# Seeding two PSUM sums from ScalarE in the second layer of a sparse graph network

## The chip, the cores and the metric

The kernel runs on one core of one Trainium2 chip. Its time is the device time of one execution, in microseconds (us). The kernel before was run three times: 926.32, 928.87 and 934.2 us, so its median is 928.87 us. A separate execution was taken by the hardware profiler; it lasted 933.13 us, and its trace spans 931.1 us from the first instruction to the last. All durations below come from that one trace.

A core has five engines that run side by side and meet at semaphores: TensorE (PE, matrix products), VectorE (DVE), ScalarE (ACT), GpSimd (POOL, which here issues the indirect transfers) and SyncE (SP, which issues plain transfers). Each runs its own list of instructions strictly in order. TensorE writes only to PSUM[...].

## The reference

Two graph layers on 3327 nodes with 512 features, each followed by a residual sum and a layer norm. Only the second one concerns the change. Here `adj` is 0/1, with some eight neighbours in a row besides the node itself:

```
type_sum = adj @ x
attn_a = sigmoid(concat(type_sum, x) @ Wa.T + ba)        # one number for each node
attn_b = sigmoid(concat(type_sum, x) @ Wb.T + bb)        # one number for each node
h = x @ W_sa
attn = row-normalised exp(-leaky_relu(s_left + s_right)) on the neighbours
x_a = attn @ h
x_b = adj @ (x @ W_gcnb) + b_gcnb
x = layernorm(x + sigmoid(attn_a * x_a + attn_b * x_b))
```

The kernel uses that sums over neighbours and projections can change places. For each node it forms a weighted sum of its neighbours' rows of `x`, with the weights `attn_a * attn`, and a plain sum of the same rows, scaled by `attn_b`. It projects the first with `W_sa` and the second with `W_gcnb`, both into one PSUM sum, and adds `b_gcnb * attn_b`.

## The kernel before

The nodes are sorted by their number of neighbours and cut into 26 tiles of 128. `CAPS[j]` says how many neighbour rows tile j holds, from 4 to 14; two of the tiles (`T0`, of 14 rows each) hold more in a shared "stair" row. After a first part that reads the adjacency matrix and does the first layer, the second layer begins about 532 us into the span.

Neighbour rows come by indirect transfers, one for each of the 226 rows and one for each of the two stairs. POOL issues them (line 615) into a ring of 42 row buffers; `gather()` issues as far as buffers are free. The own row of a node, `row1(j)`, is in SBUF from the first layer.

The loop `for i in range(NT + 3)` (lines 1150 to 1199) is a software pipeline written out by hand: in turn i, tile j is at position i of the order, j1 at i + 1, jp at i - 1 and jpp at i - 2. The order in the code is the order on each engine. In one turn:

- **ACT** takes the own score of j1 (`own_score`, line 1021), scales the plain sum of jp out of PSUM into `sp` (line 1159), copies the two transposed operands of jp out of PSUM (`sT`, line 1130), applies tanh to `za` of jpp (line 1169), does exp and tanh on the small weights of j1 (lines 1039 and 1054), finishes rows after a norm in some turns (line 1184), and at the end starts the weighted sum of j1 with the own row times its weight (`scaled_first`, line 1081).
- **PE** transposes the weighted and the plain sum of jp (`turn`, line 1128), adds the single rows of j into the PSUM sum `acc` by products with the identity (`plain_sum`, line 1118), projects jp's first half into `po` (`project`, line 1137), adds the sums of two rows of j that DVE has made, and projects jp's second half.
- **DVE** adds each row of j times its weight into `sw` (line 1097) and sums four or five pairs of rows in place (line 1099). Then come bias times gate plus projection for jpp (line 1167), the weights of j1 (lines 1032 to 1062, the last being what `scaled_first` waits for), the residual sum of jpp (line 1194) and its statistics (line 692), and after every few tiles a short chain that makes the norm's scale (lines 701 to 708).

The lines that the change touches stand thus in the loop:

```
sp = zs[jp, "sp"] = m1.tile([P, F], F32, tag="sp", name=f"sp{jp}")
nc.scalar.activation(sp, plain[jp], AF.Copy, scale=gates[jp][:, 1:2])
turn(jp, 0)
turn(jp, 1)
...
nc.vector.scalar_tensor_tensor(za, bias_g, gates[jpp][:, 1:2], proj[jpp], ALU.mult, ALU.add)
nc.scalar.activation(za, za, AF.Tanh, scale=0.5)
```

Both `acc` and `po` have two PSUM buffers that take turns from tile to tile. A product of 128x128 by 128x512 in float32 stands in the trace as two instructions (two passes).

Of the kernel before, what the change touches and what calls it, by code (L numbers as in the profile page):

```python
# [8 lines left out]
F32 = mybir.dt.float32  # L9
AF = mybir.ActivationFunctionType  # L10
ALU = mybir.AluOpType
# [3 lines left out]
P = 128  # L15
# [63 lines left out]
def sparse_pass(  # L79
# [39 lines left out]
    nc = tc.nc  # L119
    N, F = out.shape  # L120
    NP = x.shape[0]
    H, FO = a_self.shape
    KT = F // P
# [35 lines left out]
    ident = const.tile([P, P], F32, name="ident")  # L159
    ones = const.tile([P, P], F32, name="ones")  # L160
    bias0 = const.tile([P, F], F32, name="bias0")
    bias_g = const.tile([P, F], F32, name="bias_g")
# [13 lines left out]
    def place(j):  # L176

        return (0, j) if j < NG[0] else (1, j - NG[0])
# [5 lines left out]
    def row1(j):  # L184
        g, i = place(j)
        return x1[g][:, i, :]
# [468 lines left out]
    def gather():  # L655

        while waiting and waiting[0][0] - freed[0] <= RING:
            indirect(*waiting.pop(0)[1:])

    def free(j):  # L660

        freed[0] = ends_at[j]
# [78 lines left out]
    ws, accs, ws2 = {}, {}, {}  # L741
# [41 lines left out]
    def attend(j, lean, between):  # L783


        w = ws[j]
        acc = accs[j] = ps.tile([P, F], F32, tag="acc", name=f"acc{j}", bufs=2)
        if not lean:
            nc.tensor.matmul(acc, ident, bias0, start=True, stop=False)
        for s0, n, buf, o in got[j]:  # L790
            for s in range(s0, s0 + n):
                gv = buf[:, o + s - s0, 0:F].rearrange("p (h o) -> p h o", h=H)
                if s % 3 == 2:
                    for h in range(H):
                        nc.scalar.activation(gv[:, h, :], gv[:, h, :], AF.Copy, scale=w[:, s, h : h + 1])  # L795
                else:
                    nc.vector.tensor_tensor(  # L797
                        gv, gv, w[:, s, :].rearrange("p (h o) -> p h o", o=1).to_broadcast([P, H, FO]), ALU.mult
                    )
                row = buf[:, o + s - s0, 0:F]  # L800
                if lean and s == 0:
                    nc.vector.tensor_add(row, row, bias0)  # L802
                nc.tensor.matmul(  # L803
                    acc, ident, row, start=(lean and s == 0), stop=(s == CAPS[j] and j not in T0)
                )
                if s == 2:
                    between()
        if j in T0:
            gv = stair[j][:, 0:F].rearrange("p (h o) -> p h o", h=H)
            nc.vector.tensor_tensor(  # L810
                gv, gv, ws2[j].rearrange("p (h o) -> p h o", o=1).to_broadcast([P, H, FO]), ALU.mult
            )
            nc.tensor.matmul(acc, to_node, stair[j][:, 0:F], start=False, stop=True)
# [37 lines left out]
            rows_ready.append(j)  # L851

    rows_ready = []

    def put_rows():
        for j in rows_ready:
            scatter("table1", table1[:, :], own(j), row1(j), N - 1)
        rows_ready.clear()
# [3 lines left out]
    def open_pools():  # L862
        nonlocal gp, m0, ps, ring
        psf.release()
        pj.release()
        gp = ctx.enter_context(tc.tile_pool(name="gp", bufs=1))
        m0 = tc.alloc_tile_pool(name="m0", bufs=2, side="left")
        ps = ctx.enter_context(tc.tile_pool(name="ps", bufs=1, space=PSUM))
        ring = gp.tile([P, RING, ROW], F32, name="ring")

    def at_first():

        whole, part, owns = [], [], []
        for j in order0[:3]:
            n = CAPS[j] + 1 + (j in T0)
            whole, part, owns = whole + waiting[:n], part + waiting[1:n], owns + waiting[:1]
            del waiting[:n]
        assert whole[-1][0] <= RING
        waiting[:0] = owns
        for args in part:  # L880
            tc.declare_no_dep(indirect(*args[1:]), group="x rows", reason="they read rows of features only")
# [66 lines left out]
    for i in range(NT + 3):  # L948
# [10 lines left out]
        if 0 < i <= NT:  # L959
            j = order0[i - 1]  # L960
# [7 lines left out]
            if done:  # L968
                k0, scale, shift = done
# [31 lines left out]
    ps1 = ctx.enter_context(tc.tile_pool(name="ps1", bufs=1, space=PSUM, side="right"))  # L1001
# [8 lines left out]
    half = len(mid) // 2  # L1010
# [6 lines left out]
    ew, gates, sums, plain, proj, zs, stair_sum = {}, {}, {}, {}, {}, {}, {}  # L1017
# [60 lines left out]
    def scaled_first(j):  # L1078

        sw = sums[j] = m1.tile([P, F], F32, tag="sw", name=f"sw{j}")  # L1080
        nc.scalar.activation(sw, row1(j)[:, 0:F], AF.Copy, scale=ew[j][:, 0:1])  # L1081
        if j in T0:
            scaled = m1.tile([P, F], F32, tag="scaled", name=f"scaled{j}", bufs=1)
            nc.scalar.activation(scaled, stair[j][:, 0:F], AF.Copy, scale=ws2[j])
            stair_sum[j] = ps1.tile([P, F], F32, tag="stair", name=f"stair_sum{j}")
            nc.tensor.matmul(stair_sum[j], to_node, scaled, start=True, stop=True)

    def weighted(j, part):
# [11 lines left out]
        if part == 1 and j in T0:  # L1100
            nc.vector.tensor_add(sw, stair_sum[j], sw)

    def plain_sum(j, sums_of_two):
        two = paired(j)
        single, double = [(ident, row1(j)[:, 0:F])], []
        for s0, n, g, _ in got[j]:
            for i in range(n):
                if s0 + i - 1 in two:
                    double.append((ident, g[:, i, 0:F]))
                elif s0 + i not in two:  # L1110
                    single.append((ident, g[:, i, 0:F]))
        if j in T0:
            single.append((to_node, stair[j][:, 0:F]))
        if not sums_of_two:
            plain[j] = ps.tile([P, F], F32, tag="acc", name=f"acc1_{j}", bufs=2)
        rows = double if sums_of_two else single
        for i, (to, row) in enumerate(rows):
            nc.tensor.matmul(  # L1118
                plain[j], to, row, start=(not sums_of_two and i == 0),
                stop=(sums_of_two and i == len(rows) - 1),  # L1120
            )

    def turn(j, half):
# [5 lines left out]
        sT = zs[j, half] = m1.tile([P, KT, P], F32, tag=f"sT{half}", name=f"sT{half}_{j}")  # L1129
        nc.scalar.copy(sT, pt)  # L1130

    def project(j, half):
        sT, wt = zs[j, half], (wsa, wg)[half]
        if half == 0:
            proj[j] = ps1.tile([P, F], F32, tag="po", name=f"po{j}", bufs=2)
        for k in range(KT):
            nc.tensor.matmul(proj[j], sT[:, k, :], wt[:, k, :], start=(half + k == 0), stop=(half + k == KT))  # L1137

    ends = {3, 7, 11, 15, 19, 22, 24, 25}
    norm = Norm(m1, "n1", ends)  # L1140
    at_ = lambda i: order[i] if 0 <= i < NT else None
# [4 lines left out]
    weights_a(at_(0))  # L1146
    weights_b(at_(0))
    scaled_first(at_(0))
    ready, outs = None, []
    for i in range(NT + 3):  # L1150
        j, j1, jp, jpp = at_(i), at_(i + 1), at_(i - 1), at_(i - 2)
        if i > 0 and jp is not None:
            free(jp)
        gather()
        if j1 is not None:
            own_score(j1)
        if jp is not None:
# [4 lines that stand above are left out]
        if j is not None:  # L1162
            plain_sum(j, False)
            weighted(j, 0)
        if jpp is not None:
            za = zs[jpp] = m1.tile([P, F], F32, tag="za", name=f"za{jpp}", bufs=3)
            nc.vector.scalar_tensor_tensor(za, bias_g, gates[jpp][:, 1:2], proj[jpp], ALU.mult, ALU.add)  # L1167

            nc.scalar.activation(za, za, AF.Tanh, scale=0.5)  # L1169
        if jp is not None:  # L1170
            project(jp, 0)
        if j is not None:
            plain_sum(j, True)
        if j1 is not None:
            weights_a(j1)
        if j is not None:
            weighted(j, 1)
        if jp is not None:
            project(jp, 1)
        if ready:  # L1180
            k0, scale, shift = ready
            for k in range(k0, i - 2):
                z = row1(order[k])[:, 0:F]
                nc.scalar.activation(  # L1184
                    z, z, AF.Identity, scale=scale[:, k - k0 : k - k0 + 1], bias=shift[:, k - k0 : k - k0 + 1]
                )
                outs.append((own(order[k]), z))
            ready = None
        while outs and not waiting:
            scatter("out", out, *outs.pop(0), N - 1)  # L1190
        if jpp is not None:
            za = zs[jpp]
            zs[jpp] = row1(jpp)[:, 0:F]
            nc.vector.scalar_tensor_tensor(zs[jpp], za, 0.5, zs[jpp], ALU.mult, ALU.add)  # L1194
        if j1 is not None:
            weights_b(j1)
            scaled_first(j1)
        if jpp is not None:
            ready = norm.add(i - 2, zs[jpp])

# [451 lines left out]
```

## Time and profile before

| what | value | where from |
|---|---|---|
| median of the runs shown | 928.87 us | times |
| the profiled execution | 933.13 us | times |
| its span | 931.1 us | page, head |
| second layer | about 532 us to the end | trace, first own row at 531.9 us |
| PE, DVE, ACT, POOL over the span | 84%, 79%, 31%, 65% | page, part 1 |
| identity products of the own row, second layer | 52 passes, 592 to 595 ns median each | trace, line 1118 |
| bias times gate plus projection on DVE | 26, median 740 ns | trace, line 1167 |
| tanh of `za` on ACT | 26, median 630 ns | trace, line 1169 |
| SBUF to SBUF copy of 128x512 on ACT | 26, median 613 ns | trace, line 771 |
| scaled own row on ACT | 26, median 722 ns | trace, line 1081 |

How to read it: a busy share is the time in which an engine had an instruction under way, over the whole span, so a stage with its own limit is hidden in it; the second layer has to be looked at by itself. [...]Instructions of one engine overlap a little, so the distance between two starts can be shorter than a duration: what an instruction costs a full engine is the distance, not the duration.

### The profile page before, as it was taken

The page shows a single profiled execution, that of the slowest core. Times are in us where ns is not written, and L with a number is a line of the kernel's source. Part 1 is how long each engine was busy: PE and PEld are TensorE (multiplying, and loading weights), DVE is VectorE, ACT ScalarE, POOL GpSimd, SP SyncE. Part 2 cuts the span into 40 slices and gives each one's busy share as a digit, 9 for nine tenths or more (in the row PEclk, how much of TensorE's full clock was granted, in tenths as well). Part 3 has the DMA queues.
Part 4 walks back from the last instruction along what each step waited for, and adds up shares of the span by engine and source line. Part 5 has one row for each costly group of instructions (what it writes and reads, how often), then busy time and mean ns, then how long its engine had stood idle before and what let it go on. Part 6 is the DMA issues. An engine that isn't in the chain of part 4 may idle for free. (4 is left out here: it accounts for less than half of the span.)

```text
span 931.1 us, 10307 instructions
## 1 busy us (share of the span) xinstructions
PE 785.4 (84%) x2518; PEld 413.5 (44%) x2518; DVE 735.7 (79%) x2100; ACT 288.2 (31%) x820; POOL 601.9 (65%) x641
## 2 busy tenths in 40 slices
PE   4699896327899889799999749999989989999893
PEld 3477674113455444344444414444444434444341
DVE  4288878884978668879888648799989989999973
ACT  0122221002345335445464312323231222322331
POOL 6711143747877777777777477777777777777511
PEclk9799998557899979899999859999999999999997
DMA  9989989999678888797777367776777777776301
GB/s 334 362 348 372 395 319 374 379 362 407 217 221 266 244 240 265 226 366 234 215 235 227 126 191 190 198 193 190 196 197 187 192 194 193 192 193 190 146 34 38
DMA packets 73349, 224.68 MB, mean 241 GB/s; under 512 B 12736, under 2 KB 16784, under 8 KB 72384
## 3 DMA queue, kind: packets, MB, share of 16 engines
q0 software_dynamic: 46368, 153.69, 55.0%
q1 hardware_dynamic: 24256, 68.13, 19.3%
q10 hardware_dynamic: 2656, 2.10, 0.7%
q8 instruction: 23, 0.38, 0.2%
q14 instruction: 46, 0.38, 0.1%
HBM read 203.02 MB, written 31.51 MB: 252 GB/s over the span
## 5 line engine op out<-in xcount | busy, mean ns | idle before, releaser
L615 POOL DMA_INDIRECT ring<-table,srt x464 | 483.1, 1041 | 159.6 <-issue 60.3
L803 PE MATMUL acc<-ring,ident 128*128 128x512 f32 x504 | 240.8, 622 | 20.6 <-DVE ring L802 13.3
L1097 DVE SCALAR_TENSOR_TENSOR sw<-ring,e,sw 128x512 f32<-128x512 f32 x226 | 169.3, 749 | 12.1 <-ACT sw L1081 7.9
L803 PEld LDWEIGHTS acc<-ring,ident 128*128 128x128 f32 x504 | 95.3, 198 | 133.4 <-issue 74.6
L1118 PE MATMUL acc<-ring,ident 128*128 128x512 f32 x264 | 126.5, 608 | 19.6 <-DVE ring L1099 10.2
L371 PE MATMUL pf<-w,xc 128*128 128x260 f32 x416 | 105.2, 417 | 13.2 <-DVE w L311 13.2
L797 DVE TENSOR_TENSOR ring<-ring,w 128x512 f32<-128x512 f32 x176 | 111.9, 695 | 0.6
L371 PEld LDWEIGHTS pf<-w,xc 128*128 128x128 f32 x416 | 85.8, 209 | 30.1 <-DVE w L311 13.9
L1137 PE MATMUL po<-wsa,sT 128*128 128x512 f32 x208 | 95.0, 600 | 0.3 <-ACT sT L1130 0.3
L1137 PE MATMUL po<-wg,sT 128*128 128x512 f32 x208 | 93.7, 593 | 0.0
L795 ACT ACTIVATE ring<-ring,w 128x128 f32<-128x128 f32 x304 | 91.5, 391 | 0.0
L1118 PEld LDWEIGHTS acc<-ring,ident 128*128 128x128 f32 x264 | 49.8, 193 | 90.0 <-issue 44.5
L383 POOL DMA_DIRECT2D table<-row x26 | 14.3, 549 | 84.0 <-ACT st L380 82.8
L1099 DVE TENSOR_TENSOR ring<-ring 128x512 f32<-128x512 f32 x94 | 65.0, 691 | 3.2
L1169 ACT ACTIVATE za<-za 128x512 f32<-128x512 f32 x26 | 16.4, 632 | 152.9 <-DVE za L1167 152.9
L1137 PEld LDWEIGHTS po<-wsa,sT 128*128 128x128 f32 x208 | 40.2, 193 | 51.2 <-issue 48.7
L1137 PEld LDWEIGHTS po<-wg,sT 128*128 128x128 f32 x208 | 39.4, 190 | 48.8 <-issue 47.8
L402 PE MATMUL pc<-at,pow 128*32 128x512 bf16 (+1 forms) x182 | 25.0, 416 | 36.4 <-DMA at<-in_adjB 24.5
L762 ACT ACTIVATE w<-w 128x40 f32<-128x40 f32 (+10 forms) x26 | 6.2, 238 | 128.7 <-DVE w L761 128.7
L375 ACT COPY row<-pf 128x512 f32<-128x512 f32 x26 | 15.3, 587 | 97.5 <-issue 49.2
L1130 ACT COPY sT<-pt 128x512 f32<-128x512 f32 x52 | 28.4, 587 | 37.8 <-PE pt L1128 37.8
L834 PEld LDWEIGHTS pcol<-v,xt 128*128 128x128 f32 x208 | 28.1, 197 | 14.1 <-issue 11.4
(254 smaller groups left out, 940.5 us busy)
## 6 DMA issues: line engine op xcount, KB each, us to landing
at<-in_adjB SPq DMA_DIRECT2D x78, 512.0 KB, 12.0
ring<-table,srt POOLq DMA_INDIRECT x464, 3.9
table<-row POOLq DMA_DIRECT2D x26, 260.0 KB, 6.5
xc<-in_xB SPq DMA_DIRECT2D x6, 1024.0 KB, 7.2
own<-in_xo SPq DMA_DIRECT2D x1, 3640.0 KB, 44.7
own<-table SPq DMA_DIRECT2D x1, 3640.0 KB, 54.0
at<-in_adjL SPq DMA_DIRECT2D x13, 256.0 KB, 11.1
table<-in_xo SPq DMA_DIRECT2D x1, 3120.0 KB, 27.9
```

What stands on the lines that cost most here:

```text
L371: nc.tensor.matmul(pf[:, hh, :HC], xc[:, k, o : o + P], w0[:, k, hh, :], start=(k == 0), stop=(k == KT - 1))
L402: nc.tensor.matmul(pc[32 * c : 32 * c + 32, : nt * P], pow2[:, s, :], loaded[i, m], start=(s == 0), stop=(m + 1 not in ms or s == 3),)
L615: return nc.gpsimd.indirect_dma_start(out=out_, out_offset=None, in_=table, in_offset=bass.IndirectOffsetOnAxis(ap=ap, axis=0)).ins
L795: nc.scalar.activation(gv[:, h, :], gv[:, h, :], AF.Copy, scale=w[:, s, h : h + 1])
L797: nc.vector.tensor_tensor(gv, gv, w[:, s, :].rearrange("p (h o) -> p h o", o=1).to_broadcast([P, H, FO]), ALU.mult)
L803: nc.tensor.matmul(acc, ident, row, start=(lean and s == 0), stop=(s == CAPS[j] and j not in T0))
L834: nc.tensor.matmul(pcol, xt1[:, k, :], v1[:, k, :], start=(k == 0), stop=(k == KT - 1))
L1097: nc.vector.scalar_tensor_tensor(sw, g[:, i, 0:F], e[:, s : s + 1], sw, ALU.mult, ALU.add)
L1099: nc.vector.tensor_add(g[:, i, 0:F], g[:, i - 1, 0:F], g[:, i, 0:F])
L1118: nc.tensor.matmul(plain[j], to, row, start=(not sums_of_two and i == 0), stop=(sums_of_two and i == len(rows) - 1),)
L1130: nc.scalar.copy(sT, pt)
L1137: nc.tensor.matmul(proj[j], sT[:, k, :], wt[:, k, :], start=(half + k == 0), stop=(half + k == KT))
```

## The change

Both PSUM sums of a tile now begin with something that ScalarE writes into the bank, and the matrix products add to it.

- `seed_sum(j)`: ACT copies the own row into the bank of the plain sum. The identity product of the own row (one of 128x512, two passes, for each of the 26 tiles) is gone from PE's list.
- `seed_projection(k, j)`: ACT writes bias times gate into the bank of the projection, from the third tile on. For these 24 tiles the DVE instruction of line 1167 is gone, and tanh reads the projection's PSUM bank in its place. The first two tiles keep the old form; their projections are the first products in those banks, and begin them as before.
- Both seeds are issued at the end of a turn, behind `scaled_first`: the plain sum of j1, the projection of j.
- `acc` and `po` are fixed pairs of PSUM tiles taken in turn, where a pool of two buffers turned before; the first layer's sums use the same `acc` pair. The products are issued with `start=False`.

The instruction lists of the two builds differ by this on the engines: PE has 52 passes fewer, DVE 24 instructions fewer, ACT 50 more (26 copies and 24 scaled copies). POOL's and SP's lists are the same.

```
@@ attend
-        acc = accs[j] = ps.tile([P, F], F32, tag="acc", name=f"acc{j}", bufs=2)
+        acc = accs[j] = bank(j)
...
+    banks, taken = [], []
+    def bank(j):
+        taken.append(j)
+        return banks[len(taken) % 2]
...
+        banks.extend(ps.tile([P, F], F32, tag=f"acc{k}", name=f"acc{k}") for k in range(2))
...
+    def seed_sum(j):
+        plain[j] = bank(j)
+        nc.scalar.copy(plain[j], row1(j)[:, 0:F])
+
+    def seed_projection(k, j):
+        proj[j] = halls[k % 2]
+        if k >= 2:
+            nc.scalar.activation(proj[j], bias_g, AF.Copy, scale=gates[j][:, 1:2])
@@ plain_sum
-        single, double = [(ident, row1(j)[:, 0:F])], []
+        single, double = [], []
...
-                plain[j], to, row, start=(not sums_of_two and i == 0),
-                stop=(sums_of_two and i == len(rows) - 1),
+                plain[j], to, row, start=False, stop=(sums_of_two and i == len(rows) - 1), skip_group_check=True
@@ project
-    def project(j, half):
+    halls = [ps1.tile([P, F], F32, tag=f"po{k}", name=f"po{k}") for k in range(2)]
+    def project(n, j, half):
...
-            nc.tensor.matmul(proj[j], sT[:, k, :], wt[:, k, :], start=(half + k == 0), stop=(half + k == KT))
+            nc.tensor.matmul(
+                proj[j], sT[:, k, :], wt[:, k, :], start=(n < 2 and half + k == 0), stop=(half + k == KT),
+                skip_group_check=True,
+            )
@@ the loop
-            nc.vector.scalar_tensor_tensor(za, bias_g, gates[jpp][:, 1:2], proj[jpp], ALU.mult, ALU.add)
-            nc.scalar.activation(za, za, AF.Tanh, scale=0.5)
+            if i - 2 < 2:
+                nc.vector.scalar_tensor_tensor(za, bias_g, gates[jpp][:, 1:2], proj[jpp], ALU.mult, ALU.add)
+            nc.scalar.activation(za, za if i - 2 < 2 else proj[jpp], AF.Tanh, scale=0.5)
...
             weights_b(j1)
             scaled_first(j1)
+            seed_sum(j1)
+        if j is not None:
+            seed_projection(i, j)
```

More of the change, by code (lines that the diff above doesn't have):

```diff
@@ L1113, in plain_sum @@
             single.append((to_node, stair[j][:, 0:F]))
-        if not sums_of_two:
-            plain[j] = ps.tile([P, F], F32, tag="acc", name=f"acc1_{j}", bufs=2)
         rows = double if sums_of_two else single
@@ L1130, in turn @@
         nc.scalar.copy(sT, pt)
-    def project(j, half):
+    halls = [ps1.tile([P, F], F32, tag=f"po{k}", name=f"po{k}") for k in range(2)]
+    def project(n, j, half):
         sT, wt = zs[j, half], (wsa, wg)[half]
-        if half == 0:
-            proj[j] = ps1.tile([P, F], F32, tag="po", name=f"po{j}", bufs=2)
         for k in range(KT):
-            nc.tensor.matmul(proj[j], sT[:, k, :], wt[:, k, :], start=(half + k == 0), stop=(half + k == KT))
+            nc.tensor.matmul(
+                proj[j], sT[:, k, :], wt[:, k, :], start=(n < 2 and half + k == 0), stop=(half + k == KT),
+                skip_group_check=True,
+            )
     ends = {3, 7, 11, 15, 19, 22, 24, 25}
@@ L1148, in sparse_pass @@
     scaled_first(at_(0))
+    seed_sum(at_(0))
     ready, outs = None, []
@@ L1166, in sparse_pass @@
             za = zs[jpp] = m1.tile([P, F], F32, tag="za", name=f"za{jpp}", bufs=3)
-            nc.vector.scalar_tensor_tensor(za, bias_g, gates[jpp][:, 1:2], proj[jpp], ALU.mult, ALU.add)
-            nc.scalar.activation(za, za, AF.Tanh, scale=0.5)
+            if i - 2 < 2:
+                nc.vector.scalar_tensor_tensor(za, bias_g, gates[jpp][:, 1:2], proj[jpp], ALU.mult, ALU.add)
+            nc.scalar.activation(za, za if i - 2 < 2 else proj[jpp], AF.Tanh, scale=0.5)
         if jp is not None:
-            project(jp, 0)
+            project(i - 1, jp, 0)
         if j is not None:
@@ L1178, in sparse_pass @@
         if jp is not None:
-            project(jp, 1)
+            project(i - 1, jp, 1)
         if ready:
```

## The prediction

> **What bounds the kernel now.** The page's whole-span shares (PE 84%, DVE 79%) mix stages, so I took the second layer by stretches first. Columns: busy time and instructions of PE, PEld, DVE, ACT, POOL, then clock and DMA.
>
> ```profile
> 560.00:600.00 40.00, 40.00 (x111) 19.01 (x111) 31.43 (x75) 10.98 (x31) 30.86 (x31) 0.99 0.72 196
> ...
> 840.00:880.00 40.00, 37.30 (x105) 17.32 (x104) 37.18 (x83) 11.98 (x27) 29.60 (x27) 1.00 0.53 185
> ```
>
> Three engines look nearly full: PE 37 to 40 us of 40, DVE 36 to 38 from 600 us on, and POOL 31, whose indirect issues follow each other with only 0.30 us between. ACT is free for 28 us. Who waits for whom decides, so the list of waits comes next (total us, times, longest):
>
> ```profile
> DVE e L1032 <- DMA ring<-table,srt: 16.8, 3, 11.3
> DVE sw L1097 <- ACT sw L1081: 7.9, 15, 1.6
> DVE za L1167 <- PE po L1137: 6.9, 4, 3.8
> ...
> DVE own_step_l L682 <- PE to_rows L680: 1.5, 2, 1.0
> ...
> DVE e L1034 <- PE to_nodes L673: 1.3, 2, 1.0
> ```
>
> DVE's waits for gathers are three, the last (4.07 us) ending at 597.16 us. After that it waits a few us in all until the tail. **From 600 to about 890 us DVE sets the pace.** One turn shows what it pays and how close PE is; first DVE's timeline (start, duration, line):
>
> ```profile
> 848.55 1.53 DVE L1097 SCALAR_TENSOR_TENSOR sw<-ring,e,sw 128x512 f32<-128x512 f32 x2
> 850.11 0.69 DVE L1099 TENSOR_TENSOR ring<-ring 128x512 f32<-128x512 f32 x1
> 850.72 0.74 DVE L1167 SCALAR_TENSOR_TENSOR za<-bias_g,gate,po 128x512 f32<-128x512 f32 x1
> 851.38 0.23 DVE L1032 TENSOR_SCALAR e<-ring,x1b 128x9 f32<-128x9 f32 x1
> ```
>
> The instruction to be removed lasts 0.74 us, but the next starts 0.66 us after it. The same turn on PE:
>
> ```profile
> 842.44 0.60 PE L1128 MATMUL pt<-ident,sw 128*128 128x128 f32 x4
> 842.87 0.60 PE L1128 MATMUL pt<-ident,sp 128*128 128x128 f32 x4
> 843.31 1.02 PE L1118 MATMUL acc<-x1a,ident 128*128 128x512 f32 x2
> 844.17 1.88 PE L1118 MATMUL acc<-ring,ident 128*128 128x512 f32 x4
> 845.89 3.60 PE L1137 MATMUL po<-wsa,sT 128*128 128x512 f32 x8
> 849.32 3.60 PE L1118 MATMUL acc<-ring,ident 128*128 128x512 f32 x8
> 852.75 3.60 PE L1137 MATMUL po<-wg,sT 128*128 128x512 f32 x8
> 856.19 0.60 PE L1128 MATMUL pt<-ident,sw 128*128 128x128 f32 x4
> ```
>
> The starts touch: 13.75 us of PE in a turn of 13.87 us of DVE. PE is a close second and mostly waits for pair sums, but its lateness hardly reaches DVE, as shown below. Last, ACT at the turn's border:
>
> ```profile
> 841.25 0.72 ACT L1081 ACTIVATE sw<-x1a,e 128x512 f32<-128x512 f32 x1 [1.65 <-DVE e L1062]
> 841.88 0.17 ACT L1021 COPY e<-x1b 128x1 f32<-128x1 f32 x1
> 841.96 0.68 ACT L1159 ACTIVATE sp<-acc,gate 128x512 f32<-128x512 f32 x1
> 843.07 1.07 ACT L1130 COPY sT<-pt 128x512 f32<-128x512 f32 x2 [0.43 <-PE pt L1128]
> ```
>
> The chain DVE weights, `sw`, `sp`, transpose, `sT` has ACT idle ahead of it, and the seeds go right into it, between `sw` and `sp`.
>
> **What the Trainium skill says.** "ScalarE: Activation LUTs", section What ACT_TABLE_LOAD costs, prices an activation with immediate operands at 186 ns + 0.833 ns for each of 512 elements (612 ns), 93 ns more with a pointer operand, and lets neighbours overlap by 93 ns. The trace agrees: 613 ns for the copy of line 771, 722 for line 1081 and 0.63 us from its start to the next. "PSUM — Partial Sum Buffer", section Specifications (TRN2), calls ScalarE faster to PSUM than to SBUF; no ACT write to PSUM is in this trace. The same page, section The four PSUM rules, says that a ScalarE write leaves the accumulate bits alone, and that products without the first-product flag add where an earlier product set them. So the seeds add as meant, since the first layer used the `acc` banks and the first two tiles the `po` banks; the trace cannot show that.
>
> **The change part by part.**
>
> *DVE, line 1167: 24 fewer.* Each is worth 0.66 us while DVE sets the pace (from below; from above 0.77, its 0.74 and a gap of 0.03). Counted to the weights of the last tile (end of turn 24, 892.7 us), the removals fall in turns 4 to 24. Turn 4 gains nothing: DVE already waits there for tile 5's gather, and waits 0.66 us longer. Turns 5 and 6 come up against tile 7's gather: its weights start at 627.4 us, and its last gather, issued at 622 us, lands about 3.8 us later, which leaves about 1.3 us. Turns 6 and 10 also prepare the two stair tiles, where DVE waits for PE (to_nodes, to_rows); PE's place does not move, so the gain becomes wait. I keep 0.66 us for turns 5 and 6 together, and 17 of the 18 turns 7 to 24: 0.66 + 17 x 0.66 = **11.9 us**.
>
> *PE, own-row products: 52 passes fewer.* Back to back a pass takes 0.43 us (3.43 for eight), so 0.86 us a tile, 22 us in all, but not on DVE's path. Where a tile has no single row, the own row also covered the wait for `sT`: without it the projection waits for the first `sT` copy, some 0.46 us, so only about 0.4 is saved there. I count nothing until the tail. What covers this is DVE's longer turn; with that cover gone it would be worth up to 22 us (a rival below).
>
> *ACT, 50 seeds.* By line 771 and line 1081 less the overlap: 0.53 us for the copy, 0.63 for the scaled one, 1.16 us a turn. Bounds: 0.43 each if PSUM is quicker to write, and, nothing in this trace excluding it, 1.2 each if a write that meets PE's in other banks took twice as long; a cost below nothing is excluded, as they are instructions added to one queue. I take 1.16. They wait for nothing outside ACT: the bank's former reader (`sp`, `za`) is ahead on ACT itself. Queued behind them are `own_score`, `sp` and both `sT`; PE waits for `sp` at its second transposes. `sw`, which DVE waits for, is ahead of them. In the turn shown `sp` would end at 843.8 in place of 842.64, while PE would be there at 842.87 + 0.66 on the same count: 0.3 to 0.5 us of stall, against 0.86 us of product saved. ACT goes from 9 to 13 us of each 40 to about 15. Tanh no longer waits for DVE (152.9 us of ACT's waits, which held nothing up), and its PSUM read changes nothing on the path.
>
> *Gathers.* POOL issues one each 1.25 to 1.5 us without pause until 849 us. The lead of landing over use is 6 us at positions 9 and 11 and grows to 38 us at the last. DVE will have gained some 4 us at position 11 and 12 at the end, so gathers stay hidden. SP's and POOL's lists don't move.
>
> *Tail.* In the last turns PE has the word: its passes run from 884 us to 915.3 without a gap over 0.5 us. After tile 24's weights (884.2 us, gain 11.2 there) PE's second transposes follow about 1.1 us later than they do now (0.66 that DVE gained and PE did not, the rest stall for `sp`); then PE saves 0.86 and 0.4 on the last two own rows; then tanh starts 0.84 us earlier, as line 1167 (915.47 to 916.31) is gone. Together 1.0 us: 11.2 + 1.0 = **12.2 us at the end**; I round to 12.
>
> Banks in place of pool buffers: same two buffers, same readers, nothing. The sum stands against the profiled execution: 933.13 - 12 = 921.1 us. That run is 0.46% above the median of the runs shown, so for the median: 928.87 - 12 = **917 us**.
>
> **The rivals.**
>
> 1. *Dearer seeds.* What late seeds cost DVE is only at the two stair tiles, where it waits for PE, and once in the tail: three places, each 2 x (s - 0.58) for s us a seed. At s = 1.2 that takes 3.7 us and leaves a gain of 8.3 (921); at s = 2, 3.5 (925). For: ACT's idle time is not where the seeds stand. Against: line 771.
> 2. *The gathers hold the end.* POOL has no pause; if landing still set DVE's pace past position 7, the gain would be the tail's 1 us: 928. Against: the lead of 6 to 38 us.
> 3. *PE sets the pace.* It is fuller than DVE in the stretches; then 26 x 0.86 = 22 us, 907. Against: DVE waits for PE only some 4 us before the tail.
> 4. *Slower.* The same queue as in 1: PE stuck at its transposes behind `sp`. From 6 x (s - 0.58) = 12, that is s = 2.6 us, the loss outweighs the gain; at s = 3, 2.5 us slower (931). It needs over four times line 771.
>
> That the seeds are not added would change the result, not the time.
>
> **How the numbers follow.** A measurement of this kernel tells about 1% (9.3 us) from no change. Forecast, 8 to 15 us gained: 0.62. Rival 1, 3 to 8 us: 0.17. Rival 2: 0.07. Rival 3 or a mix of it, 15 to 22 us: 0.08. Rival 4: 0.06. The forecast's own range is 914 to 921. Leaving out gains over 17 and under 3 us (0.05 + 0.07 + 0.06): **912 to 926**. Faster by over 1%: nine tenths of the forecast, all of rival 3 and a little of rival 1, 0.68; within 1%: 0.26; slower: 0.06.
>
> **What would show it.** Right: DVE's starts around the place of line 1167 close up (pair sum to weights 0.61 us), turns of equal tiles about 0.66 us shorter from 640 us on, small PE gaps ahead of the second transposes, ACT seeds of 0.6 to 0.7 us. Wrong: seeds over 1 us, DVE waits for gathers past 650 us, or new DVE waits for ACT or PE beyond the stair tiles.

## The result and the profile after

The changed kernel takes 916.57 us (median of four runs, 914.84 to 920.24), the kernel before 930.84 (926.32 to 934.2). The ratio on record is 0.9875, with a 95% interval from 0.9847 to 0.9904: 1.25% faster, 11.6 us (8.9 to 14.2). It is not the quotient of these two medians, which lie 14.3 us apart. The profiled execution took 920.24 us, where the prediction's sum gave 921.1; its span is 918.1 us.

One thing must be known for the totals below: 9 of the 12 experiments fell on occasions when every kernel, the one before too, took 1050 to 1115 us ("stalled occasions" below), so their totals can't be set beside the ones above.

The stretches of the changed kernel, with the prediction's columns:

```profile
560.00:600.00 40.00, 39.76 (x112) 18.58 (x110) 30.13 (x70) 13.52 (x35) 30.86 (x31) 1.00 0.70 195
...
840.00:880.00 40.00, 37.01 (x104) 17.10 (x103) 36.90 (x92) 16.98 (x40) 31.33 (x29) 1.00 0.56 191
```

PE and DVE are as full as before, and only ACT has grown, in these two stretches from 11 or 12 us of 40 to 14 or 17. Busy shares can't tell that the stage runs faster; the turns behind them are shorter. DVE's waits:

```profile
DVE e L1039 <- DMA ring<-table,srt: 19.5, 3, 11.6
DVE x1a L1214 <- ACT za L1189: 7.7, 1, 7.7
DVE sw L1104 <- ACT sw L1088: 7.2, 11, 1.7
DVE x1b L1214 <- ACT za L1189: 2.6, 1, 2.6
DVE own_step_l L682 <- PE to_rows L680: 1.5, 2, 1.0
...
DVE e L1041 <- PE to_nodes L673: 0.4, 1, 0.4
```

The waits for tanh (7.7 and 2.6 us) stand in the tail, at 897.20 and 904.04 us, where line 1167 waited for PE before. The three waits for gathers all lie before the weights of position 5. From there to the tail DVE waits a few us in all, as before, mostly for `sw` (in the whole layer 7.2 us in 11 times, before 7.9 in 15) and at the stair tiles. The place of the removed instruction on DVE:

```profile
826.55 1.53 DVE L1104 SCALAR_TENSOR_TENSOR sw<-ring,e,sw 128x512 f32<-128x512 f32 x2
828.11 0.69 DVE L1106 TENSOR_TENSOR ring<-ring 128x512 f32<-128x512 f32 x1
828.72 0.23 DVE L1039 TENSOR_SCALAR e<-ring,x1a 128x10 f32<-128x10 f32 x1
```

From the pair sum to the weights it is 0.61 us, where before it was 1.27 (850.11 to 851.38): the 0.66 us are gone and nothing has come in. The border of the turn on ACT and on PE:

```profile
819.89 0.58 ACT L1114 COPY acc<-x1a 128x512 f32<-128x512 f32 x1
820.40 0.68 ACT L1120 ACTIVATE po<-bias_g,gate 128x512 f32<-128x512 f32 x1
821.02 0.17 ACT L1028 COPY e<-x1a 128x1 f32<-128x1 f32 x1
821.10 0.68 ACT L1179 ACTIVATE sp<-acc,gate 128x512 f32<-128x512 f32 x1
```

```profile
821.19 0.60 PE L1144 MATMUL pt<-ident,sw 128*128 128x128 f32 x4
821.83 0.66 PE L1144 MATMUL pt<-ident,sp 128*128 128x128 f32 x4
822.33 1.02 PE L1135 MATMUL acc<-ring,ident 128*128 128x512 f32 x2
823.19 3.60 PE L1153 MATMUL po<-wsa,sT 128*128 128x512 f32 x8
```

The first two lines are the seeds, which ScalarE writes into the PSUM buffers where TensorE then adds its products. They take 1.13 us from start to start (819.89 to 821.02). The second transposes follow the first after 0.64 us in place of 0.43: that is PE's wait for `sp`, 0.21 us in this turn. In 15 of the 26 turns there is none (0.44 us from the first to the second).

### The profile page after: what moved, and what is told of

Same layout as the page of the kernel before. It is cut to its first block, busy times and chain, and to the rows that moved or that the text cites. A ratio compares the mean times of both kernels' runs of the same rounds, so it can differ in the third digit from the quotient of the medians.

```text
span 918.1 us, 10223 instructions
## 1 busy us (share of the span) xinstructions
PE 762.2 (83%) x2466; PEld 402.4 (44%) x2466; DVE 718.6 (78%) x2076; ACT 316.9 (35%) x870; POOL 598.4 (65%) x641
## 5 line engine op out<-in xcount | busy, mean ns | idle before, releaser
L371 PE MATMUL pf<-w,xc 128*128 128x260 f32 x416 | 103.9, 413 | 13.1 <-DVE w L311 13.1
L383 POOL DMA_DIRECT2D table<-row x26 | 14.3, 550 | 85.1 <-ACT st L380 82.7
L1046 ACT ACTIVATE e<-e 128x9 f32<-128x9 f32 (+10 forms) x26 | 5.5, 211 | 146.4 <-DVE e L1044 146.4
L828 ACT COPY xt<-x1t 128x512 f32<-128x512 f32 x26 | 15.2, 585 | 62.8 <-PE x1t L822 62.8
```

Source lines behind the costliest of these rows:

```text
L371: nc.tensor.matmul(pf[:, hh, :HC], xc[:, k, o : o + P], w0[:, k, hh, :], start=(k == 0), stop=(k == KT - 1))
```

## The experiments

The yardstick is the turn: the distance between the starts of the last weight instruction (line 1062 before, 1069 in the changed kernel) of successive tiles, worked out from the traces. Turn 12 runs from the weights of the tile at position 12 of the order to those of position 13. Here are five turns in which nothing stalled in any of the traces listed, in us:

```
turn                            12     14     15     17     18     sum
before                        12.44  15.10  16.03  13.82  15.71   73.10
before, again (e9)            12.44  15.09  16.04  13.82  15.72   73.11
changed                       11.54  14.64  15.64  12.93  14.71   69.46
projection seed only (e1)     11.73  14.38  15.63  12.93  14.75   69.42
sum seed only (e2)            12.25  15.06  16.03  13.82  15.58   72.74
seeds behind tanh (e10)       11.54  14.65  15.63  12.93  14.70   69.45
each seed twice (e7)          11.51  14.39  15.63  13.16  14.73   69.42
fewer pair sums (e11)         11.00  13.87  14.20  13.16  14.11   66.34
```

**Which half carries the gain (e1, e2, e5, e12).** Each takes one half of the change alone. e1 and e5 are the same kernel, as are e2 and e12.

```
# e1, e5: the own row is a product again, no seed_sum
-        single, double = [], []
+        single, double = [(ident, row1(j)[:, 0:F])], []
...
# e2, e12: bias times gate is on DVE again, no seed_projection
-            if i - 2 < 2:
-                nc.vector.scalar_tensor_tensor(za, bias_g, gates[jpp][:, 1:2], proj[jpp], ALU.mult, ALU.add)
-            nc.scalar.activation(za, za if i - 2 < 2 else proj[jpp], AF.Tanh, scale=0.5)
+            nc.vector.scalar_tensor_tensor(za, bias_g, gates[jpp][:, 1:2], proj[jpp], ALU.mult, ALU.add)
+            nc.scalar.activation(za, za, AF.Tanh, scale=0.5)
```

> Only the projection is seeded; the own row stays a product on PE. If DVE sets the pace, the 24 removed DVE instructions carry the gain: 11 to 12 us faster than the kernel before, within 1 us of the changed kernel, and DVE's turns 0.66 us shorter. If PE sets the pace (rival 3), the 22 us of own-row products carry it and most of the gain is gone here: 0 to 4 us faster than before.

> Only the plain sum is seeded; bias times gate stays on DVE. If DVE sets the pace: 0 to 1 us faster than before, although PE has 52 passes (22 us) fewer. If PE sets the pace: at least 8 us faster, towards 22.

> The projection's seed alone once more, on another occasion, for its total. DVE's pace: 10 to 12 us faster than before, within 1.5 us of the changed kernel. PE's pace: 0 to 4 us.

> Only the plain sum is seeded, for its total on an occasion where the kernel before takes about 930 us. DVE's pace: 0 to 1 us faster than before although PE has 52 passes (22 us) fewer, and DVE's turns as long as before. PE's pace: at least 8 us faster.

All four fell on stalled occasions. The totals of three missed on both readings: e1 came to 1.0188 (1.0082 to 1.0295) and e5 to 1.0227 (1.0146 to 1.0308) of the kernel before, e2 to 1091.85 us against 1078.33, without a ratio. e12's 0.9895 (0.9831 to 0.9959) would, taken alone, speak for PE's pace, but the medians of all its runs lie only 2.3 us apart (1074.85 and 1077.12). The turns do tell: with the projection's seed alone five turns are 3.68 us shorter (3.78 in e5), 0.74 each, as with the whole change (3.64); with the sum's seed alone 0.36, 0.07 each (0.14 in e12), although PE has 0.86 us less in each. So in the steady part the DVE instruction is the gain. For the total of the halves there is no measurement to go by.

**Whether the place and the price of the seeds count (e3, e4, e6, e10; e7).** e3, e6 and e10 are one kernel; e4 is the changed kernel beside e3.

```
# e3, e6, e10: seeds directly behind tanh (and not behind scaled_first)
             nc.scalar.activation(za, za if i - 2 < 2 else proj[jpp], AF.Tanh, scale=0.5)
+        if j1 is not None:
+            seed_sum(j1)
+        if j is not None:
+            seed_projection(i, j)
...
# e7: each seed twice, in the change's place
-        nc.scalar.copy(plain[j], row1(j)[:, 0:F])
+        for _ in range(2):
+            nc.scalar.copy(plain[j], row1(j)[:, 0:F])
...
-        if k >= 2:
+        for _ in range(2 if k >= 2 else 0):
```

> Both seeds move on ScalarE from between sw and sp to just behind the tanh of jpp, where ScalarE is idle for some 5.6 us. If the seeds' delay of sp costs PE 0.3 to 0.5 us a turn, and DVE sees it only at the stair tiles and in the tail: PE's gaps ahead of the second transposes go, and the end comes 1 to 2 us earlier than in the changed kernel. If the place of the seeds doesn't matter: the same within 0.5 us.

> The changed kernel again, beside the other three on the same chip: 11 to 13 us faster than before by either theory; it is the base for the differences.

> The seeds behind the tanh once more, for its total. If the delayed sp is seen only in the tail and at the stair tiles: 1 to 2 us faster than the changed kernel, so 13 to 14 faster than before, with equal turns of DVE. If the place doesn't matter: 12.

> Each seed is written twice, in the place where the change puts it: 1.15 us more a turn between sw and sp. By the prediction's count, three places that see it, 3.5 us of the gain go (8 to 9 left), and DVE's turns away from the stair tiles stay as they are. If ScalarE's time counted in every turn: 26 x 1.15 = 30 us, far slower than before. If it is hidden everywhere: no change.

> The seeds behind the tanh, on an occasion where the kernel before takes about 930 us again. If the delayed sp is seen only in the tail and at the stair tiles: 1 to 2 us faster than the changed kernel (13 to 14 faster than before) and PE's waits for sp gone. If the place doesn't matter: 12.

On the stalled occasions e3 came to 1.0113 (1.0063 to 1.0163), e4 to 1.006 (1.0006 to 1.0113), e6 to 1.0066 (1.0011 to 1.0121), e7 to 1.0134 (1.0005 to 1.0264): e4 missed its 11 to 13 us, and the others what was expected of them. e10, on a quiet one, gave 914.88 us against 929.38, 0.9843 (0.9818 to 0.9869). That interval overlaps the changed kernel's. Its trace says why no more can be claimed. PE's wait for `sp`, in the list of waits of its weight loads, first before, then in the changed kernel, then in e10:

```profile
PEld pt L1128 <- ACT sp L1159: 4.6, 4, 1.3
```

```profile
PEld pt L1144 <- ACT sp L1179: 11.3, 9, 3.3
```

```profile
PEld pt L1144 <- ACT sp L1179: 4.1, 5, 1.5
```

The wait falls back to what it was before, as expected. But from the weights of position 8 to those of position 25 both take the same, 230.24 and 230.25 us, and from position 24 to the end 46.00 and 46.27. Of the 3.4 us between the two spans 2.8 are there already at the second layer's first weights (546.51 and 543.75 us). So the expected 1 to 2 us did not appear: PE's wait is real, and nothing waits for PE there. e7 points the same way: its five turns are those of the changed kernel, and the turn that prepares the second stair tile (10) takes 16.03 us against 15.92, where the prediction's count had 1.2 us more. What doubling does to the first stair tile and to the tail can't be read, as stalls lie in both.

**Whether PE's new room can be used (e8, e11).** One kernel, run twice, with the seeds as in e10.

```
-        left = 4 + (CAPS[j] >= 13)
+        left = 4 + (CAPS[j] >= 13) - (CAPS[j] in (8, 9))
```

> Seeds behind the tanh, and in tiles of 8 or 9 rows DVE makes one pair sum fewer (0.61 us less) while PE adds two single rows in place of one sum (0.86 us more, of which the wait for sT hides some in tiles of 8). If DVE sets the pace and PE has the room that the own row left: 4 to 8 us faster than the changed kernel. If PE is now equally full: no gain, or slower by up to 0.25 us for each of the nine tiles.

> One pair sum fewer in tiles of 8 or 9 rows, seeds behind the tanh. The turns of these tiles were 0.5 to 1.1 us shorter in the other trace, so 4 to 8 us faster than the changed kernel, 16 to 20 faster than before; less where the gathers (0.6 us of lead at position 11 of the changed kernel) become the wait. If PE has become the bound: the total stays at 12 to 14 faster than before.

e8 came to 1.0217 (1.0127 to 1.0306) on a stalled occasion, a miss. e11 gave 907.0 us against 929.38, 0.9775 (0.9749 to 0.9801): 20.9 us faster than before (18.5 to 23.3), just above the 16 to 20 expected, and faster than e10 beside it, with intervals apart. From position 8 to 25 it takes 222.52 us against 230.25. It is the best version found. One turn is longer than in e10: 17.07 us against 15.92 in turn 10, where DVE now waits 2.5 us for the transfer of the second stair row, so there the transfers have become the wait. PE's waits for DVE's pair sums, before the change, in e10 and in e11:

```profile
PEld acc L1118 <- DVE ring L1099: 25.1, 25, 4.5
```

```profile
PEld acc L1135 <- DVE ring L1106: 29.7, 28, 1.9
```

```profile
PEld acc L1135 <- DVE ring L1106: 9.6, 13, 1.9
```

PE has used up most of the room that it spent waiting for DVE. But 25.1 us of such waits were there before the change too, so it is not shown that this step needs the seeds at all: fewer pair sums without them was not tried. That the own row's 0.86 us of PE pays here, as room for DVE's work, is possible and open.

**What the stalls are (e9).**

> The kernel before, with a profile, on the occasion of the experiments, where it took 1078 to 1083 us against 931 earlier. If the pauses of TensorE (DVE waiting 28 to 32 us for a projection long issued, in the turn of the third tile) belong to the chip, the same turn is some 50 us long here too, and undisturbed turns are as long as in the first trace (12.44, 13.82 us). If ScalarE's seeds bring the pauses in, they are absent here.

e9 met a quiet occasion (929.73 us, turns as in the first trace), so it doesn't answer the question. In the stalled traces the other engines wait for TensorE's results. PE and DVE in e3:

```profile
645.71 3.60 PE L1153 MATMUL po<-wg,sT 128*128 128x512 f32 x8
```

```profile
686.88 0.75 DVE L1188 SCALAR_TENSOR_TENSOR za<-bias_g,gate,po 128x512 f32<-128x512 f32 x1 [32.33 <-remote]
```

The last eight passes of a projection stand in the trace up to 649 us, yet DVE gets their sum only at 686.88; "remote" means that the profile finds no instruction that released it. As the ends of passes are modelled, the trace can't say whether TensorE itself stood still or its signal came late. The same turn takes 46.9 to 50.5 us in e1 to e8 and 36.4 in e12, against 9.2 to 9.6 in the quiet traces, and mean granted clocks are 0.845 to 0.865 against 0.91. Long totals don't need the seeds: the kernel before was slow there too (medians 1077 to 1083 us), and 80 us or more of the time lost is lost before the first seed, as the first weights of the second layer stand at 628 to 658 us there, against 539 to 547 in the quiet traces. But every version with the projection's seed for which a ratio is on record came out 0.6 to 2.3% slower than the kernel before there, so the gain is shown for quiet occasions alone. Why stays open, as the kernel before has no trace from a stalled one.

## Why the prediction was right

The forecast's mechanism held: DVE sets the pace, one instruction leaves each turn, and the turn is shorter by the distance of two starts, not by the duration.

- **24 DVE instructions at 0.66 us.** From position 8 to 25, 17 turns, 241.70 us (241.31 in e9) became 230.24: 0.65 to 0.67 us a turn. The upper bound, 0.77, would have given 13.1 for the 11.46 measured. Single turns range from 0.23 to 1.00. Those whose waits stayed the same (13, 19, 20, 23, 24) gained 0.65 or 0.66; turns 9, 12, 16 and 17, with 0.89 to 0.95, also lost a wait of 0.2 us for `sw`. The five turns of the yardstick happen to be above the mean, at 0.73: 12 and 17 are of that kind, 18 gained 1.00, and 14 and 15 less (0.46 and 0.39), for reasons not looked into.
- **Turn 4 loses its gain to tile 5's gather.** It does: DVE waits there 7.25 us, before 4.07. That is 3.2 longer and not 0.66; DVE comes there earlier than reckoned, and all of it is lost. From the first weights to those of tile 5 it is 54.53 us before and 54.26 after.
- **Stair tiles.** Too dark: of turns 5 and 6 I kept 0.66 us, of turn 10 nothing. Turn 5 is 0.68 shorter, turn 6 0.83, turn 10 0.23; against e9, turns 5 and 6 together are 1.0 shorter in place of 1.5. DVE's waits for PE there (own_step and to_nodes) did not grow: 2.8 us before (2.5 in e9), 1.9 after.
- **Seeds at 1.16 us a turn.** 1.13 measured. PE's wait for `sp` grew by 6.7 us in all. That is 0.26 a turn, against 0.3 to 0.5, but it isn't spread over the turns as the forecast had it: 15 of the 26 have no wait, and one alone, at 603.7 us, has 3.3.
- **Three places that pay 2 x (s - 0.58).** This is the term that was mis-sized, in rivals 1 and 4: e7 shows 0.1 us at the second stair tile for 1.15 us of delay, e10 no gain from taking the delay away. So break-even should lie higher than the 2.6 us a seed that I gave; no run measures it.
- **Own rows on PE count for nothing until the tail.** Right in the steady part: 0.07 us a turn in e2.
- **Tail 1.0 us.** From position 24 to the end 47.17 us became 46.00, 1.2 us; e9 has 48.09 there, so this term is known to about 1 us only. The stall for `sp` that I set against the saving is not there in e10's reading: without it the tail is as long.
- **Gathers stay hidden.** They do after position 7, more narrowly than I reckoned. With 3.9 us from issue to landing (page, part 6), the lead at position 11 went from 6.2 to 0.8 us, and DVE has gained only 2.5 there; the gathers themselves began 1.4 us later and took 315.0 us from first to last against 313.3. At the last position 22 us of the 38 are left.

The sum is near in part by luck, as two differences cancel: from the first weights to the end, the profiled execution gained 14.5 us (13.5 against e9) where I counted 12, and that second layer began 1.5 us later than in the trace before. The later start is not the change's doing as far as the traces show: the first weights stand at 545.01 and 542.63 us before, at 546.51, 543.75 and 539.10 in the changed kernel, e10 and e11. The totals don't choose between 12 and 14: the ratio on record says 11.6 us, the two medians 14.3.

## What to carry to other kernels

Price a removed instruction by the distance to the next start on its engine, and count it only in the turns in which that engine waits for nobody. Work taken from an engine that runs second paid next to nothing by itself here (0.07 us a turn for 0.86 us of PE). What paid was to give the second engine some of the first one's work: 6.3 us more by the ratios of e10 and e11 (medians 914.88 and 907.0), once PE got rows that DVE had summed. A new wait that shows in the trace costs only if somebody waits for the one that waits.

## What the runs showed of the hardware

In the changed kernel ScalarE wrote to PSUM a little faster than to SBUF: medians of 577 ns for the copy of 128x512 into PSUM and 613 into SBUF, and of 677 against 722 for the one with a scale. But that depends on where the instruction stands: behind tanh the same copy into PSUM took 620 ns in e10 and 617 in e11, no less than into SBUF, and the one with a scale 711 and 710. Why is not shown. Tanh took 615 ns from PSUM against 630 from SBUF. And on some occasions the engines that wait for TensorE's results got them up to 33 us late (e7), and totals of the same kernel rose from about 930 us to between 1057 and 1106.
